# Where the copy of the softmax denominators' row stands in ScalarE's order, inside the block of values and keys

## The chip, the cores and the metric

The kernel runs on one core of a Trainium2 chip. Its engines work side by side, each through its own list of instructions in order: TensorE (PE in the profile, its weight loads PEld) multiplies matrices into PSUM, ScalarE (ACT) applies functions and copies, VectorE (DVE) does elementwise work, GpSimd (POOL) the same[...], and SyncE (SP) issues transfers. They wait for one another by semaphores. The metric is the device time of one execution in microseconds. Before the change it is 2444.21 us, the median of 3 runs (2444.15 to 2444.86).

## The reference

Two layers, each followed by a residual and a layer norm, on x of 16 batches x 1024 nodes x 256 channels. The first layer makes a weighted adjacency from the channel means, its queries from that graph, and runs attention with 4 heads of 64:

```python
c_adj = jnp.mean(fea, axis=1)                       # fea = x transposed
diff = c_adj[:, None, :] - c_adj[:, :, None]
A = jnp.abs(jnp.abs(jax.nn.sigmoid(diff) - 0.5) - 0.5) * 2.0
A_s = (A + jnp.transpose(A, (0, 2, 1))) * 0.5
Wg = adj[None, :, :] * A_s
g = jax.nn.relu(jnp.einsum('bcn,bnm->bcm', fea, Wg) * para.reshape(1, C, N))
q = ...                                             # g, split in heads
kv = (x @ kv_w)...                                  # keys and values, split in heads
attn = jax.nn.softmax(jnp.einsum('bhnd,bhmd->bhnm', q, k) * scale, axis=-1)
out = jnp.einsum('bhnm,bhmd->bhnd', attn, v)
x = _layernorm(x + out)
```

The second layer aggregates x over the normalised adjacency, applies two matmuls with batch norms and a relu, and ends in the same residual and layer norm. The change concerns the first layer alone.

## The kernel before, in words

The first layer is a software pipeline over units of attention. A unit is one batch, one pair of heads, one half of the queries (512) and one chunk of 128 keys: 32 units a batch. `scores` (L1053) multiplies keys by queries into PSUM and ScalarE takes the exponent (L1058); `outputs` (L1074) multiplies values by it, while VectorE adds the exponents up in `acc` (L1082, L1084). Two units form a burst, so a batch b has bursts u = 0 to 15. The loop over bursts writes out by hand the order of the instructions of TensorE, ScalarE, VectorE and SP: nothing is moved by a scheduler afterwards, and an instruction at the head of an engine's list holds all behind it.

Between the bursts the loop places the work that prepares batch b + 1 and finishes batch b - 1. It is kept in lists of steps, and `run(list, k)` emits the next k of them.

- `steps` holds values (L995) and keys (L982) in turn: `values(0), keys(0,0), values(1), keys(0,1), values(2), keys(1,0), values(3), keys(1,1)`. Each fills one PSUM tile of 128 x 512 with four or two matmuls, and is then copied to SBUF: keys by ScalarE (L986), values 1 and 3 by ScalarE and values 0 and 2 by VectorE (L1000).
- `side` holds the graph weights in 8 chunks of 128 x 1024: `weights_abs` (L827, ScalarE, |c_m - c_n|), `weights_tanh` (L832, ScalarE) and `weights_adj` (L836, VectorE, times adj).
- `sums` holds `normalise`: four matmuls with ones (L1122) add the partial exponents over the partitions into a PSUM tile `den`, ScalarE copies it to `drow` (L1128), and SP stores its four rows (L1130) and loads them back as columns (L1135). The column's reciprocal (L1143) later scales the attention output on GpSimd (L1149, L1150).
- `rows_of` holds the four SP loads (L1113) that bring an attention output back in rows.

Values, keys and `den` take their PSUM tiles in turn from one pool of two buffers: the tile after next waits until the copy out of the present one is done. So `den` sits between keys(0,0) and values(1), and keys(0,1) reuses the buffer that `den` has left.

The block of values and keys is burst u = 0 of batches 1 to 14 (in batch 0 the lists are empty, and batch 15 takes another branch). It emits seven of the eight values and keys, with the denominators of the second pair of heads of batch b - 1 after the second:

```python
for i in range(7):
    if b:
        run(steps, 1)
        run(side, (2, 3, 2, 3, 2, 2, 99)[i])
    if i == 1:
        run(sums, 1)
        run(rows_of, 1)
```

When the block starts, seven entries of `side` have been emitted in bursts 9 to 15 of the batch before. The next are tanh 3 and abs 4 (with i = 0), then tanh 4, adj 0 and abs 5 (with i = 1), then tanh 5 and adj 1, and so on.

Of the kernel before, what the change touches and what calls it, by code (L numbers as in the profile page):

```python
# [515 lines left out]
def fast_path(  # L516
# [218 lines left out]
    with (  # L735
# [36 lines left out]
        def load_rest():  # L772
            for n in range(2, NCH, 2):
                nc.sync.dma_start(adj_s[:, n : n + 2, :], adj_src[:, n : n + 2, :])
                if n == 2:
                    load_x(1)
            nc.sync.dma_start(para_s, para.rearrange("o (c p) i j -> p (o c) (i j)", p=P))
# [395 lines left out]
        def run(fs, k):  # L1173
            for f, a in fs[:k]:
                f(*a)
            del fs[:k]
# [135 lines left out]
        with tc.manual_schedule(  # L1312
            engines={
                mybir.EngineType.PE, mybir.EngineType.Activation, mybir.EngineType.DVE,
                mybir.EngineType.SP,
            }
        ):


            first, steps, side = prologue(0)  # L1320
            run(first, 5)
            load_rest()
            next_first, next_steps, next_side = prologue(1)
            for i in range(8):
                run(steps, 1)
                if i > 3:
                    run(side, 2)
                if i == 6:
                    run(next_first, 1)
                    load_squares(1, 0)  # L1330
            run(side, 99)
            for n in range(NCH):
                run(steps, 1)
                if n in (1, 5):
                    run(next_first, 1)
                if n == 1:
                    load_squares(1, 1)
                if n:
                    run(next_side, 3)
            for _ in range(8):  # L1340
                run(next_steps, 1)
                run(next_side, 1)
            full, sums, late = [], [], []
            rows_of = []

            def back(j):

                for i in bursts[j]:
                    outputs(i)
                b, pr, qh, m = units[bursts[j][-1]]  # L1350
                if m == NCH - 1 and qh == 1:
                    sums.append((normalise, (b, pr)))
                    for q in range(2):
                        full.append((residual, (b, pr, q)))
                    if pr == PAIRS - 1:
                        for f in (statistics_x1, finish_x1):
                            for ns in (range(NCH // 2), range(NCH // 2, NCH)):
                                late.append((f, (b, ns)))

            last, before_last = {}, {}  # L1360
            for u, todo in (
                (6, (load_x1l, 0)), (7, (load_weights,)), (9, (degrees,)), (10, (row_of_degrees,)),
                (11, (transpose_weights, 0)), (12, (transpose_weights, 1)),
                (13, (add_identity,)), (14, (scale_adjacency, 0)),
            ):
                last.setdefault(u, []).append((todo[0], todo[1:]))
            for f, places in (
                (transpose_adjacency, (9, 11, 13, 15, 17, 19, 21, 23)),
                (load_adjacency_squares, (6, 9, 9, 11, 13, 15, 17, 19)),
                (adjacency_columns, (11, 13, 14, 16, 18, 20, 22, 24)),  # L1370
            ):
                for m, u in enumerate(places):
                    where = before_last if u < PERB else last
                    where.setdefault(u % PERB, []).append((f, (m,)))
            for u, n in ((9, 6), (10, 7)):
                before_last.setdefault(u, []).append((adjacency_rows, (n,)))
            for i in range(4):
                ns = range(2 * i, 2 * i + 2)
                last.setdefault(8 + i, []).append((statistics_x1, (B - 2, ns)))
            for u, ns in ((13, range(2)), (14, range(2, 5)), (15, range(5, NCH))):  # L1380
                last.setdefault(u, []).append((finish_x1, (B - 2, ns)))
            last[15].append((load_x1l, (1,)))
            for j in range(len(bursts)):
                b, u = j // PERB, j % PERB
                for i in bursts[j]:
                    scores(i)
                if u == 0:
                    steps, side = next_steps, next_side
                    next_first, next_steps, next_side = [], [], []
                if j:  # L1390
                    back(j - 1)
                if u in (5, 9, 13):
                    run(rows_of, 1)
                if u == 5 and b + 2 < B:
                    load_x(b + 2)
                    next_first, next_steps, next_side = prologue(b + 2)
                if b == B - 1:
                    if u == 0:
                        run(sums, 1)
                        run(rows_of, 1)  # L1400
                    elif u in (2, 13):
                        run(full, 2)
                    elif u == 8:
                        run(sums, 1)
                    elif u == 3:
                        late.clear()
                elif u == 0:
                    for i in range(7):
                        if b:
                            run(steps, 1)  # L1410
                            run(side, (2, 3, 2, 3, 2, 2, 99)[i])
                        if i == 1:
                            run(sums, 1)
                            run(rows_of, 1)
                elif u < 4:
                    if u == 1:
                        run(full, 2)
                    else:
                        run(late, 1)
                    run(side, 99)  # L1420
                elif u == 4:
                    p = st[b + 1]["graph"]["p"]
                    keys_last = steps[:1] if b else []
                    del steps[: len(keys_last)]
                    p[1]()
                    run(keys_last, 1)
                    run(late, 2)
                    p[2]()
                    p[3]()
                elif u == 8:  # L1430
                    p = st[b + 1]["graph"]["p"]
                    p[6]()
                    run(next_first, 1)
                    run(sums, 1)
                    if b == B - 2:
                        adjacency_diagonal()
                        for n in range(6):
                            adjacency_rows(n)
                    p[7]()
                    p[5]()  # L1440
                    p[4]()
                elif u < 8:
                    st[b + 1]["graph"]["between"](u)
                else:
                    if u == 9 and b + 2 < B:
                        load_squares(b + 2, 0)
                    if u == 11:
                        run(full, 2)
                    if u == 12:
                        run(next_first, 1)  # L1450
                        if b + 2 < B:
                            load_squares(b + 2, 1)
                    if u == 15:
                        run(next_first, 1)
                    run(next_side, 1)
                if b == B - 2:
                    run(before_last.get(u, []), 9)
                if b == B - 1:
                    run(last.get(u, []), 9)
            j = len(bursts)  # L1460
            back(j - 1)
            for m in range(NCH):
                if m == 0:
                    for k in range(3, NCH):
                        scale_adjacency(k)
                elif m < 4:
                    adjacency_sums(m - 1)
                elif m == 4:
                    adjacency_sums(3)
                aggregate_first(m)  # L1470
                if m == 1:
                    run(sums, 1)
                if m == 4:
                    run(full, 2)
            late.clear()
            x_last = st.pop(B - 1)["x"]
            last_statistics, last_apply = layernorm_steps(x_last, f"l0_{B - 1}")
            last_statistics()
# [583 lines left out]
```

## Time and profile before

| what | value |
|---|---|
| median of 3 runs | 2444.21 us |
| the profiled execution | 2444.04 us |
| its span on the core | 2442.3 us |
| TensorE busy | 2401.4 us, 98% of the span |
| VectorE busy | 1860.5 us, 76% |
| ScalarE busy | 1239.0 us, 51% |
| GpSimd busy | 462.8 us, 19% |
| granted TensorE clock | 0.997 |

The span is what the trace covers; the profiled execution's own time lies 1.7 us above it. Each line of a profile group gives the source line, the engine, the operation, out<-in with shapes and count, then the busy time, the mean of one in ns, and the idle time just before them with what ended it. In the time line the first column is the start in us, the second the stretch that the merged instructions cover. A time line's merged rows of one engine may overlap a little, since a matmul's end is modelled. TensorE's matmuls in 32 bits appear as two records each.

### The profile page before, as it was taken

How to read it: one execution, taken by the hardware profiler on the slowest of the kernel's cores; microseconds unless marked ns; L12 is line 12 of the kernel's file. 1: busy time of each engine (PE TensorE's matmuls, PEld its weight loads, DVE VectorE, ACT ScalarE, POOL GpSimd, SP SyncE). 2: the span in 40 equal slices, each digit the busy share in tenths (PEclk: the TensorE clock that was granted, in tenths of full speed). 3: DMA queues.
4: the chain of work that ended last, by engine and by line, in shares of the span. 5: the costliest groups of instructions: out<-in, count | busy, mean ns of one | idle time of the engine just before them, and what ended most of it. 6: DMA issues, size and time to landing. Idle time of an engine off the chain costs nothing.

```text
span 2442.3 us, 32486 instructions
## 1 busy us (share of the span) xinstructions
PE 2401.4 (98%) x12294; PEld 1015.7 (42%) x12294; DVE 1860.5 (76%) x2561; ACT 1239.0 (51%) x1539; POOL 462.8 (19%) x467
## 2 busy tenths in 40 slices
PE   9999999999999999999999999999999999999996
PEld 5343443443434434434344343344444444444444
DVE  5688878878888788788888888955566556479978
ACT  7376675765765756657657667420110111144568
POOL 0021112111211211112112112422122122010026
PEclk9999999999999999999999999999999999999999
DMA  5124232332242332332322326321221221265558
GB/s 164 40 40 87 56 50 70 69 52 65 41 81 57 49 79 61 53 70 53 66 62 40 87 46 92 90 103 69 86 103 69 88 102 69 86 222 177 180 202 357
DMA packets 437877, 221.96 MB, mean 91 GB/s; under 512 B 361552, under 2 KB 411216, under 8 KB 431568
## 3 DMA queue, kind: packets, MB, share of 16 engines
q1 hardware_dynamic: 418400, 169.20, 28.2%
q0 software_dynamic: 2528, 33.57, 3.3%
q10 hardware_dynamic: 16784, 17.04, 2.1%
q8 instruction: 98, 1.61, 0.3%
q14 instruction: 67, 0.55, 0.1%
HBM read 136.06 MB, written 83.69 MB: 90 GB/s over the span
## 4 chain that ended last, share of the span: by engine, by line
PE 86%; DVE 9%; ACT 2%; DMA 1%; issue 1%; POOL 0%; POOLq 0%; DVEq 0%; ACTq 0%
PE ps L1053 18%; PE po L1074 18%; PE pgb L885 7%; PE b_agg L1558 4%; PE pga L885 4%; PE c_agg L1558 4%; PE pk L982 4%; PE b_o L1766 3%; PE pv L995 3%; PE a_agg L1558 2%; PE b_h L1590 2%; PE pgc L885 2%; PE pgd L885 2%; PE c_o L1766 2%; PE a_o L1766 2%; PE c_h L1590 2%
## 5 line engine op out<-in xcount | busy, mean ns | idle before, releaser
L1058 ACT ACTIVATE p<-ps 128x1024 f32<-128x1024 f32 x512 | 497.2, 1021 | 183.8 <-PE ps L1053 146.0
L1084 DVE TENSOR_TENSOR acc<-acc,p 128x1024 f32<-128x1024 f32 x384 | 499.9, 1302 | 53.4 <-ACT p L1058 28.5
L1053 PE MATMUL ps<-qT,kT 64*64 64x512 f32 x4096 | 488.1, 592 | 0.3 <-ACT p L1058 0.3
L1074 PE MATMUL po<-p,v 64*64 64x512 f32 x4096 | 485.3, 589 | 0.0
L1149 POOL TENSOR_TENSOR o<-o,r_all 128x512 f32<-128x512 f32 x62 | 94.8, 1540 | 1162.3 <-DVE r_all L1143 989.0
L1074 PEld LDWEIGHTS po<-p,v 64*64 64x64 f32 x4096 | 158.2, 133 | 281.2 <-issue 274.3
L1053 PEld LDWEIGHTS ps<-qT,kT 64*64 64x64 f32 x4096 | 151.5, 133 | 286.8 <-issue 249.1
L836 DVE SCALAR_TENSOR_TENSOR wg<-wg,adj_s 128x1024 f32<-128x1024 f32 x128 | 149.6, 1216 | 17.6 <-ACT wg L832 17.6
L827 ACT ACTIVATE wg<-crow,ccol 128x1024 f32<-128x1024 f32 x128 | 146.8, 1147 | 0.0
L832 ACT ACTIVATE wg<-wg 128x1024 f32<-128x1024 f32 x128 | 136.0, 1062 | 0.9
L995 PE MATMUL pv<-kvw_s,xT 128*128 128x256 f32 x512 | 125.1, 387 | 0.0
L982 PE MATMUL pk<-xT,kvw_s 128*128 128x512 f32 x256 | 121.9, 598 | 3.1 <-ACT drow L1128 3.1
L995 PEld LDWEIGHTS pv<-kvw_s,xT 128*128 128x128 f32 x512 | 95.7, 191 | 50.3 <-issue 14.2
L895 ACT ACTIVATE qT<-qT 128x512 f32<-128x512 f32 x60 | 37.4, 630 | 156.1 <-DVE qT L898 145.3
L885 PE MATMUL pgb<-wg,S 128*128 128x512 f32 x240 | 111.0, 605 | 0.0
L885 PE MATMUL pga<-wg,x 128*128 128x512 f32 x240 | 109.6, 599 | 0.7 <-ACT qT L908 0.7
L1558 PE MATMUL a_agg<-ahT,x1l 128*128 128x512 f32 x240 | 108.1, 593 | 0.7 <-ACT agg L1300 0.7
L1150 POOL TENSOR_TENSOR x<-x,o 128x512 f32<-128x512 f32 x62 | 107.8, 1749 | 2.4
L1558 PE MATMUL b_agg<-aT,x1S 128*128 128x512 f32 x240 | 107.9, 592 | 0.0
L656 ACT COPY p_agg<-a_agg 128x512 f32<-128x512 f32 x15 | 8.8, 585 | 183.4 <-PE a_agg L1558 183.4
L692 POOL TENSOR_TENSOR x1S<-x1l 128x512 f32<-128x512 f32 x15 | 19.4, 1297 | 353.6 <-PE c_agg L1558 349.6
L1082 DVE TENSOR_TENSOR acc<-p,p 128x1024 f32<-128x1024 f32 x64 | 77.3, 1208 | 7.5 <-ACT p L1058 7.5
(230 smaller groups left out, 3468.5 us busy)
## 6 DMA issues: line engine op xcount, KB each, us to landing
h<-hw POOLq DMA_DIRECT2D x16, 2048.0 KB, 6.7
hl<-h SPq DMA_DIRECT2D x32, 1024.0 KB
x<-x ACTq DMA_DIRECT2D x16, 1024.0 KB
x1l<-x SPq DMA_DIRECT2D x16, 1024.0 KB
xf<-x SPq DMA_DIRECT2D x16, 1024.0 KB
o<-oS SPq DMA_DIRECT2D x62, 256.0 KB
o<-o SPq DMA_DIRECT2D x248, 64.0 KB
x<-in_x_dram SPq DMA_DIRECT2D x15, 1024.0 KB
```

Source lines behind the costliest of these rows:

```text
L827: nc.scalar.activation(w, s["crow"], AF.Abs, bias=s["ccol"][:, n : n + 1])
L832: nc.scalar.activation(w, w, AF.Tanh, scale=0.5)
L836: nc.vector.scalar_tensor_tensor(w, w, 1.0, adj_s[:, n, :], op0=ALU.subtract, op1=ALU.mult)
L885: nc.tensor.matmul(ps, left, right, start=(start and i == 0), stop=(i == NCH // 2 - 1), skip_group_check=True,)
L982: nc.tensor.matmul(ps, kvw_s[:, c, kc * P : (kc + 1) * P], s["xT"][:, c, hs], start=(c == 0), stop=(c == CC - 1),)
L995: nc.tensor.matmul(pt[:, j * C : (j + 1) * C], s["xT"][:, c, n * P : (n + 1) * P], kvw_s[:, c, C : 2 * C], start=(c == 0), stop=(c == CC - 1),
L1053: nc.tensor.matmul(ps[kh * D : (kh + 1) * D, hd * HALF : (hd + 1) * HALF], kT[r, pr, ks], qT[r, pr, qh * HALF : (qh + 1) * HALF], start=Tr ...
L1058: nc.scalar.activation(p, ps, AF.Exp)
L1074: nc.tensor.matmul(g["po"][kh][hd * D : (hd + 1) * D, :], s["v"][r, m, h * D : (h + 1) * D], p[r, hd * HALF : (hd + 1) * HALF], start=(m = ...
L1084: nc.vector.tensor_add(g["acc"], g["acc"], p)
L1558: nc.tensor.matmul(ps, left, right, start=(start and i == 0), stop=(i == NCH // 2 - 1), skip_group_check=True,)
L1766: nc.tensor.matmul(ps, left, right, start=(start and i == 0), stop=(i == 1), skip_group_check=True,)
```

## The change

The row copy of the block of values and keys, on ScalarE, is emitted after the tanh of chunk 4 and before the abs of chunk 5; until now it came after that abs. The block's second step emits one entry of `side` (tanh 4) in place of three, then come the denominators and the loads of rows, and then the two entries held back (adj 0, abs 5).

```diff
                     for i in range(7):
                         if b:
                             run(steps, 1)
-                            run(side, (2, 3, 2, 3, 2, 2, 99)[i])
+                            run(side, (2, 1, 2, 3, 2, 2, 99)[i])
                         if i == 1:
                             run(sums, 1)
                             run(rows_of, 1)
+                            run(side, 2 if b else 0)
```

Engine by engine, the built programs differ in ScalarE's order alone, in 14 places, one for each of the batches 1 to 14: `tanh 4, abs 5, drow, v` becomes `tanh 4, drow, abs 5, v`. No instruction is added or taken away.

## The prediction

> **What bounds the kernel now.** I read the page first: busy shares, the chain that ended last, then the group of the matmuls beside the edit.
>
> ```profile
> PE 2401.4 (98%) x12294; PEld 1015.7 (42%) x12294; DVE 1860.5 (76%) x2561; ACT 1239.0 (51%) x1539; POOL 462.8 (19%) x467
> PE 86%; DVE 9%; ACT 2%; DMA 1%; issue 1%; POOL 0%; POOLq 0%; DVEq 0%; ACTq 0%
> L982 PE MATMUL pk<-xT,kvw_s 128*128 128x512 f32 x256 | 121.9, 598 | 3.1 <-ACT drow L1128 3.1
> ```
>
> TensorE is busy for 98% of the span and is 86% of the last chain, so a microsecond that TensorE stands still is, very nearly, a microsecond of the kernel. ScalarE has time to spare; it matters only where TensorE waits for it. The third line is such a place: the key matmuls wait for the copy that the change moves. Asked for that copy alone, the trace says who waited for it (us, times):
>
> ```profile
>   PEld pk L982: 8.8, 14
>   PE pk L982: 3.1, 14
> ```
>
> Fourteen waits: one in the block of values and keys of each of the batches 1 to 14. 8.8/14 = 0.63 us is the idle time of the weight load, 3.1/14 = 0.22 us that of the multiplier. Neither is yet the true loss, because matmul ends are modelled and loads overlap. For that I read the time line of one such block (batch 7), first up to the wait:
>
> ```profile
> 730.28 1.99 PE L995 MATMUL pv<-kvw_s,xT 128*128 128x256 f32 x8
> 732.12 1.88 PE L982 MATMUL pk<-xT,kvw_s 128*128 128x512 f32 x4
> 733.93 1.06 PE L1122 MATMUL den<-acc,ones 128*32 128x512 f32 x8
> 734.03 0.59 ACT L986 COPY kT<-pk 128x512 f32<-128x512 f32 x1 [1.05 <-PE pk L982]
> 734.52 1.06 ACT L832 ACTIVATE wg<-wg 128x1024 f32<-128x1024 f32 x1
> 734.92 1.99 PE L995 MATMUL pv<-kvw_s,xT 128*128 128x256 f32 x8
> 735.47 1.14 ACT L827 ACTIVATE wg<-crow,ccol 128x1024 f32<-128x1024 f32 x1
> 736.51 0.57 ACT L1128 COPY drow<-den 128x512 f32<-128x512 f32 x1
> 736.98 0.60 ACT L1000 COPY v<-pv 128x512 f32<-128x512 f32 x1
> ```
>
> and then after it:
>
> ```profile
> 737.14 0.30 PEld L982 LDWEIGHTS pk<-xT,kvw_s 128*128 128x128 f32 x2 [0.62 <-ACT drow L1128]
> 737.14 1.98 PE L982 MATMUL pk<-xT,kvw_s 128*128 128x512 f32 x4 [0.22 <-ACT drow L1128]
> 737.46 1.07 ACT L832 ACTIVATE wg<-wg 128x1024 f32<-128x1024 f32 x1
> 738.96 1.89 PE L995 MATMUL pv<-kvw_s,xT 128*128 128x256 f32 x8
> 739.16 0.58 ACT L986 COPY kT<-pk 128x512 f32<-128x512 f32 x1 [0.63 <-PE pk L982]
> 740.47 0.41 PEld L982 LDWEIGHTS pk<-xT,kvw_s 128*128 128x128 f32 x2
> 740.69 1.88 PE L982 MATMUL pk<-xT,kvw_s 128*128 128x512 f32 x4
> 742.40 1.89 PE L995 MATMUL pv<-kvw_s,xT 128*128 128x256 f32 x8
> ```
>
> The denominators' matmuls (den) end at 734.99. ScalarE is then inside a tanh until 735.58, goes on to an abs, and copies the row only at 736.51 to 737.08. The next key matmuls reuse den's PSUM buffer, and start at 737.14, 0.06 us after that copy. All that time the row stood ready.
>
> **What the Trainium skill says.** "TensorE: Matmul & The Clock Gate", Step-by-step: matmuls stay in program order, and the next weight load is pulled ahead of the matmul in flight. The trace agrees: the undisturbed pair loads at 740.47, 0.22 us before its matmul at 740.69; the held pair loads and starts together at 737.14, so its load is bare. "ScalarE: Activation LUTs", Table sets: cheap functions are in every set, and tanh is with exp. So copy, tanh and abs in another order should want no table load; the trace has such sequences back to back without a gap (kT copy 734.03, tanh 734.52, abs 735.47). The same page, What ACT_TABLE_LOAD costs, has back-to-back activations overlap by about 93 ns: here the tanh ends at 735.58 and the abs starts at 735.47, 0.11 us.
>
> **The change part by part.**
> Removed and added: no instruction; counts and tiles stay. On ScalarE, one order changes 14 times: tanh of chunk 4, abs of chunk 5, row copy becomes tanh of chunk 4, row copy, abs of chunk 5. The multiplication by adj that the code moves with the abs is VectorE's, and has no other VectorE instruction to change places with; VectorE, TensorE and the DMA queues keep their orders. Batch 0 has no such block, batch 15 takes another branch: both cost nothing.
>
> The copy: it takes the abs's place at 735.47 and ends near 736.05, 1.04 us sooner. It needs den, done at 734.99, so it does not wait (0.48 us spare). Its release reaches TensorE at about 736.11. Without a wait, the key matmuls would follow their values as the first pair of the block does: 730.28 to 732.12, 1.84 us. So they start at 734.92 + 1.84 = 736.76, with a load 0.22 us ahead at 736.54, still 0.43 us after the release. The wait is gone.
>
> What that is worth: the held step took 737.14 - 734.92 = 2.22 us, the free one 1.84: 0.38 us. The held key matmuls then take 738.96 - 737.14 = 1.82 us to the next values, the free ones 742.40 - 740.69 = 1.71: 0.11 us for the bare load. Together 0.49 us. The blocks of batch 1 (154.77, 156.98, 158.81) and batch 14 (1411.78, 1413.99, 1415.81) give 2.21 and 1.83 or 1.82 in the same places, so 0.48 to 0.50. I take 0.49: 14 x 0.49 = 6.9 us. The bounds are the profile's two rows, 3.1 us (multiplier's idle time) and 8.8 us (load's); the lower leaves out the bare load and the modelled end, the upper counts 0.2 us in which the load would have rested anyway.
>
> The abs of chunk 5: it starts about 0.47 us later (735.94). Queued behind it are the copy of values (v), the tanh of chunk 5, the next kT copy. But abs plus row copy is the same sum either way, so v still starts near 736.98, where its own matmuls have just ended (734.92 + 1.99 = 736.91), and the tanh at 737.46. So VectorE gets chunk 5 no later. Hidden: nothing to pay.
>
> Next possible waits, with TensorE 0.49 us ahead: the third values' load moves from 738.53 to 738.04, and needs v, done at 737.58: 0.40 us spare after 0.06 of signal. The kT copy follows its matmuls (ScalarE idles 0.63 us for them); its tanh ends at 738.53, the keys then at about 738.6: 0.1 us spare. Third keys, load at 739.98, need that kT copy, done near 739.25. From there every ScalarE and VectorE step waits for TensorE, and moves with it.
>
> DMAs: the copy's four stores, four column loads and the four loads of rows queued behind them on SP start up to 1.04 us sooner (stores from 737.11 to about 736.07). SP has nothing else waiting there; the reciprocal at 748.18 that uses them is held by VectorE's own order. Worth nothing here.
>
> The batches are in lockstep, 96.70 us apart, so what a block gains is not given back by a fixed clock; no TensorE wait for a DMA is listed after the start.
>
> Sum: the profiled execution took 2444.04 us (span 2442.3 and 1.7 around it); minus 6.9 is 2437.1. The median of the runs is 0.17 above it: 2444.21 - 6.9 = 2437.3.
>
> **The rivals.**
> Only the multiplier's named idle time comes back: 14 x 0.22 = 3.1 us, 2441.1. For it: that is how the profile prices the wait. Against: the starts of the matmuls, which are not modelled, show 0.49.
>
> The wait moves on: the next values wait for v, or the keys for kT, by what was gained: 2444.2. For it: the smallest of these margins is 0.1 us. Against: that smallest one delays ScalarE alone; TensorE's own margins are 0.4 us or more.
>
> Slower: the row copy, now ahead of the abs, finds den unfinished and stops ScalarE's queue, as in the middle of each batch, where the copy waited up to 4.1 us. Place: row copy at 735.47. v comes 1.51 us after it, lasts 0.60, signals in 0.06, and is needed at 738.04, so it hurts from a den later than 735.87, eats the gain by 736.36, and costs 0.2% (0.35 us in each block) from 736.7. At 737.0: 14 x (1.13 - 0.49) = 9 us, 2453. Against: den ends at 734.99, 0.9 us before the first of these points, and its place on TensorE is unchanged.
>
> That the order doesn't change can be left out: it is ScalarE's own program order.
>
> **How the numbers follow.** About 0.2%, 4.9 us, is what a measurement of this kernel can tell from no change. The forecast (0.43 to 0.62 us a block) has 0.84; its own range is 2435.5 to 2438.2. Multiplier's share only 0.07, wait moved on 0.06, slower 0.03. Faster by over 0.2%: 0.84 and a little of the partial cases, 0.86; within: 0.11; slower: 0.03. The range runs from the whole load wait, 2444.2 - 8.8 = 2435.4, to the multiplier's share alone, 2441.1.
>
> **What would show it.** In the profile after, no key matmul waits for drow; values to keys takes about 1.84 us, keys to the next values 1.71; the batch period falls from 96.70 to 96.2; ScalarE's row copy starts right after the tanh with no wait for den. Wrong: a wait of values for v or of drow for den in these blocks, or a period that shrinks by 0.2.

## The result, and the profile after

The changed kernel takes 2437.33 us, the median of 9 runs (2436.02 to 2437.80), against 2444.15 us, the median of 9 runs of the kernel before (2442.96 to 2444.86). The ratio is 0.9971 with a 95% interval of 0.9961 to 0.9982, so 6.8 us less, and clear of no change. The forecast was 2437.3 us. The profiled execution took 2437.42 us, its span 2435.6 us, 6.7 us less than the span before.

The page after: the engines' busy time, the chain that ended last, and the group of the key matmuls.

```profile
PE 2397.9 (98%) x12294; PEld 1016.6 (42%) x12294; DVE 1860.0 (76%) x2561; ACT 1239.0 (51%) x1539; POOL 462.9 (19%) x467
PE 89%; DVE 9%; DMA 1%; issue 1%; ACT 0%; SPq 0%; POOL 0%; DVEq 0%; POOLq 0%; ACTq 0%
L982 PE MATMUL pk<-xT,kvw_s 128*128 128x512 f32 x256 | 120.4, 592 | 0.0
```

The same work is done: counts are equal, and the busy time of ScalarE is the same to 0.1 us. What went is the idle time ahead of the keys, 3.1 us before and 0.0 now, and with it ScalarE's 2% of the last chain. That share is not the gain. In every block before, the chain ran through tanh, abs and row copy, 1.06 + 1.03 + 0.48 = 2.57 us in batch 7, or 36 us in 14 blocks, and the span lost 6.7: TensorE was at work beside them for most of that time. In the trace after, nobody waits for the row copy.

The time line of the block of batch 7, from den on (columns as before: start, stretch, engine, line, operation, and in brackets the idle time before it):

```profile
730.18 1.06 PE L1122 MATMUL den<-acc,ones 128*32 128x512 f32 x8
730.77 1.06 ACT L832 ACTIVATE wg<-wg 128x1024 f32<-128x1024 f32 x1
731.17 1.99 PE L995 MATMUL pv<-kvw_s,xT 128*128 128x256 f32 x8
731.73 0.58 ACT L1128 COPY drow<-den 128x512 f32<-128x512 f32 x1
732.19 1.16 ACT L827 ACTIVATE wg<-crow,ccol 128x1024 f32<-128x1024 f32 x1
732.79 0.41 PEld L982 LDWEIGHTS pk<-xT,kvw_s 128*128 128x128 f32 x2
733.01 1.88 PE L982 MATMUL pk<-xT,kvw_s 128*128 128x512 f32 x4
733.24 0.58 ACT L1000 COPY v<-pv 128x512 f32<-128x512 f32 x1
733.71 1.08 ACT L832 ACTIVATE wg<-wg 128x1024 f32<-128x1024 f32 x1
734.72 1.89 PE L995 MATMUL pv<-kvw_s,xT 128*128 128x256 f32 x8
734.92 0.58 ACT L986 COPY kT<-pk 128x512 f32<-128x512 f32 x1
```

From values 1 to the keys it is now 733.01 - 731.17 = 1.84 us, where it was 2.22; from the keys to values 2 it is 734.72 - 733.01 = 1.71 us, where it was 1.82. The weight load of the keys stands 0.22 us ahead of its matmul again (732.79), hidden behind the values. That is 0.49 us in this block.

It recurs in all of them. The chain that ended last shows the first graph product of each batch; these are those of batches 2, 3 and 4, in the kernel before and then in the changed one:

```profile
178.03 3.63 PE pga L885 x8
274.73 3.63 PE pga L885 x8
371.42 3.63 PE pga L885 x8
```

```profile
176.74 3.63 PE pga L885 x8
272.94 3.63 PE pga L885 x8
369.14 3.63 PE pga L885 x8
```

96.70 us a batch have become 96.20. Fourteen times 0.49 us is 6.9 us, and so it is over all the blocks together: from the first graph product of batch 1 to that of batch 15 the chain takes 1435.04 - 82.11 = 1352.93 us before and 1427.36 - 81.31 = 1346.05 after. The spans differ by 6.7 us. The rest is not the change's: in this pair of executions the graph product of batch 1, ahead of all the blocks, already starts 0.8 us sooner (81.31 for 82.11), and what follows the blocks takes about a microsecond more.

### The profile page after: what moved, and what is told of

Read it like the earlier page. It is cut to its first block, busy times and chain, and to the rows that moved or that the text cites. A ratio compares the mean times of both kernels' runs of the same rounds, so it can differ in the third digit from the quotient of the medians.

```text
span 2435.6 us, 32486 instructions
## 1 busy us (share of the span) xinstructions
PE 2397.9 (98%) x12294; PEld 1016.6 (42%) x12294; DVE 1860.0 (76%) x2561; ACT 1239.0 (51%) x1539; POOL 462.9 (19%) x467
## 4 chain that ended last, share of the span: by engine, by line
PE 89%; DVE 9%; DMA 1%; issue 1%; ACT 0%; SPq 0%; POOL 0%; DVEq 0%; POOLq 0%; ACTq 0%
PE ps L1053 18%; PE po L1074 18%; PE pgb L885 7%; PE b_agg L1559 5%; PE pv L995 4%; PE pga L885 4%; PE c_agg L1559 4%; PE pk L982 4%; PE b_o L1767 3%; PE a_agg L1559 2%; PE b_h L1591 2%; PE pgc L885 2%; PE pgd L885 2%; PE c_o L1767 2%; PE a_o L1767 2%; PE c_h L1591 2%
```

## The experiments

All times are medians; each ratio is against runs of the kernel before on the same chip.

| kernel | what differs from before | us (runs) | before, us | ratio, 95% interval |
|---|---|---|---|---|
| changed | row copy ahead of abs 5 | 2437.33 (9) | 2444.15 | 0.9971 [0.9961, 0.9982] |
| e1_odd | the same in 7 of the 14 blocks | 2440.72 (21) | 2444.14 | 0.9986 [0.9979, 0.9992] |
| e2_later | row copy behind tanh 5 | 2458.94 (5) | 2444.14 | 1.0061 [1.0047, 1.0075] |
| e3_earlier | row copy ahead of tanh 4 | 2437.35 (8) | 2444.14 | 0.9972 [0.9962, 0.9983] |
| e4_own_buffer | order of before, den in another PSUM pool | 2437.23 (9) | 2444.14 | 0.9973 [0.9963, 0.9983] |
| e5_both | changed order and e4's pool | 2437.21 (8) | 2443.97 | 0.9972 [0.9962, 0.9983] |

**Half of the blocks.** The changed order in the odd batches alone:

```diff
-                            run(side, (2, 3, 2, 3, 2, 2, 99)[i])
+                            run(side, (2, 1 if b % 2 else 3, 2, 3, 2, 2, 99)[i])
                         if i == 1:
                             run(sums, 1)
                             run(rows_of, 1)
+                            run(side, 2 if b % 2 else 0)
```

> The new order in the odd batches alone, 7 blocks of 14. Theory (each block's key matmuls wait for the row copy, 0.49 us a block, and nothing else changes): 7 x 0.49 = 3.4 us below before, about 2440.7; the listed wait of keys for drow is left 7 times, and the distance from block to block alternates between 96.2 and 96.7. Rival (a shift of the whole schedule, won or lost once): 2437.3 or 2444.2.

Measured: 3.4 us less than before. Who waited for the row copy, and the starts of the graph products of batches 2 to 5 in the chain that ended last:

```profile
  PEld pk L982: 4.4, 7
  PE pk L982: 1.6, 7
```

```profile
176.71 3.63 PE pga L885 x8
273.40 3.63 PE pga L885 x8
369.60 3.63 PE pga L885 x8
466.30 3.63 PE pga L885 x8
```

The distances are 96.69, 96.20, 96.70: long where the order is the old one, short where it is new. The gain is made block by block, about half a microsecond in each, and is kept. The rival, a shift won once, falls.

**One place later.** The row copy behind the tanh of chunk 5:

```diff
-                            run(side, (2, 3, 2, 3, 2, 2, 99)[i])
+                            run(side, (2, 4, 1, 3, 2, 2, 99)[i])
```

> The row copy one place later than before, after the tanh of chunk 5 (the copy of values 1 stays right behind it). Theory (TensorE pays one for one for every us that the row copy is late): tanh before it starts at abs + 1.04, the copy 0.97 us later than before, so keys 0.97 us later in each block: 14 x 0.97 = 13.6 us above before, about 2457.8. Rival (the chunk of weights that comes earlier for VectorE counts too): less than 10 us above.

Measured: 14.8 us more than before, 1.2 us beyond the theory's figure. Batch 7 in the time line:

```profile
740.93 1.99 PE L995 MATMUL pv<-kvw_s,xT 128*128 128x256 f32 x8
741.48 1.14 ACT L827 ACTIVATE wg<-crow,ccol 128x1024 f32<-128x1024 f32 x1
742.65 1.06 ACT L832 ACTIVATE wg<-wg 128x1024 f32<-128x1024 f32 x1
743.62 0.57 ACT L1128 COPY drow<-den 128x512 f32<-128x512 f32 x1
744.24 1.99 PE L982 MATMUL pk<-xT,kvw_s 128*128 128x512 f32 x4 [1.31 <-ACT drow L1128]
```

The tanh starts 1.17 us after the abs, not 1.04. It reads what the abs writes, and 742.65 is after the abs ends at 742.62, where instructions that don't depend on each other overlapped by 0.1. The block of batch 7 in the kernel before, further on, already had such a pair, 1.18 us apart:

```profile
739.64 1.15 ACT L827 ACTIVATE wg<-crow,ccol 128x1024 f32<-128x1024 f32 x1
740.82 1.06 ACT L832 ACTIVATE wg<-wg 128x1024 f32<-128x1024 f32 x1
```

An exponent that doesn't read the abs ahead of it starts 1.04 us after it there (706.56 to 707.60), so it is not the abs, nor a change of function alone, that takes the overlap away. So the row copy comes 743.62 - 741.48 = 2.14 us after the start of the abs, where it was 1.04 (735.47 to 736.51): 1.10 us later. The keys start 744.24 - 740.93 = 3.31 us after the values, where it was 2.22: 1.09 us later. Fourteen times 1.09 is 15.3 us, and from the first graph product of batch 1 to that of batch 15 the chain is 15.2 us longer than before (81.60 to 1449.74); the medians differ by 14.8. TensorE pays one for one once it is held. The theory's 0.97 was off by the overlap that a dependent pair doesn't have. The rival, that VectorE's earlier chunk pays some of it back, isn't seen.

**One place earlier.** The row copy ahead of the tanh of chunk 4:

```diff
-                            run(side, (2, 3, 2, 3, 2, 2, 99)[i])
+                            run(side, (2, 0, 2, 3, 2, 2, 99)[i])
                         if i == 1:
                             run(sums, 1)
                             run(rows_of, 1)
+                            run(side, 3 if b else 0)
```

> The row copy one place earlier than in the changed kernel, ahead of the tanh of chunk 4. Theory: ScalarE is free for it at 734.5 and must wait for den until 735.0, so 0.4 to 0.5 us of ScalarE's queue is lost; tanh, abs and the copy of values 1 come 0.5 us later than in the changed kernel, that copy ends near 738.1 where its buffer's next weight load is wanted at 738.04: a hold of 0.1 us and a bare load of 0.1, so 0.1 to 0.25 us a block are given back: 2438.7 to 2440.8, and the page lists a wait of values for v. Rival (earlier is never worse, TensorE has slack there): 2437.3, no such wait.

Measured: 2437.35 us, the same as the changed kernel. The theory missed. Batch 7:

```profile
731.16 0.59 ACT L1128 COPY drow<-den 128x512 f32<-128x512 f32 x1 [0.43 <-PE den L1122]
731.64 1.06 ACT L832 ACTIVATE wg<-wg 128x1024 f32<-128x1024 f32 x1
732.60 1.14 ACT L827 ACTIVATE wg<-crow,ccol 128x1024 f32<-128x1024 f32 x1
732.85 1.88 PE L982 MATMUL pk<-xT,kvw_s 128*128 128x512 f32 x4
733.64 0.57 ACT L1000 COPY v<-pv 128x512 f32<-128x512 f32 x1
734.26 1.79 PEld L995 LDWEIGHTS pv<-kvw_s,xT 128*128 128x128 f32 x8 [0.36 <-ACT v L1000]
734.57 1.89 PE L995 MATMUL pv<-kvw_s,xT 128*128 128x256 f32 x8
```

Everything on ScalarE came as foretold: it waits 0.43 us for den, v ends at 734.21, and the load of values 2 starts at 734.26, held for 0.36 us where the free one rests for 0.24. So it is late by 0.12 us, and yet the matmuls of values 2 start 734.57 - 732.85 = 1.72 us after the keys, as in the changed kernel. The free load starts 0.43 us ahead of its matmul here (738.53 against 738.96 in the kernel before) and lasts 0.19; the late one starts 0.31 us ahead, still in the shadow of the keys. The profile lists this wait in all 14 blocks, 5.1 us in total, and none of it shows in the time. The theory had taken the start of the undisturbed load for the latest that costs nothing.

**Another buffer, the old order.** In the blocks of batches 1 to 14, the tile of den comes from the pool of the attention outputs:

```diff
-            den = tile_s("den_last")[:, H0] if last else tile_t(f"den_{k}")
+            tile = tile_o if pr == 1 and b < B - 2 else tile_t
+            den = tile_s("den_last")[:, H0] if last else tile(f"den_{k}")
```

> ScalarE's order as before; the denominators' PSUM tile of these blocks alone is taken from the pool of the attention outputs, which rests there, so no key matmul needs the buffer that the row copy frees. Theory (the loss is the buffer's reuse alone): the whole gain comes back, 14 x 0.49 = 6.9 us, and up to 0.1 us a block more, since values 1 no longer reuse the keys' buffer and their load need not be bare: 2435.9 to 2437.3. Rival (the gain comes from the row's transfers that start sooner, or from the later abs): none of these moves here, 2444.2.

Measured: 6.9 us less than before. Batch 7 (the row copy is line 1129 here):

```profile
730.81 1.06 PE L1123 MATMUL den<-acc,ones 128*32 128x512 f32 x8
731.81 1.59 PEld L995 LDWEIGHTS pv<-kvw_s,xT 128*128 128x128 f32 x8 [0.84 <-issue]
731.81 1.99 PE L995 MATMUL pv<-kvw_s,xT 128*128 128x256 f32 x8
732.36 1.14 ACT L827 ACTIVATE wg<-crow,ccol 128x1024 f32<-128x1024 f32 x1
733.40 0.57 ACT L1129 COPY drow<-den 128x512 f32<-128x512 f32 x1
733.64 1.88 PE L982 MATMUL pk<-xT,kvw_s 128*128 128x512 f32 x4
735.36 1.89 PE L995 MATMUL pv<-kvw_s,xT 128*128 128x256 f32 x8
```

The abs is ahead of the row copy as in the kernel before, and the copy still runs when the keys start: 1.83 us after the values, 1.72 to the next. ScalarE's order, the abs's place and the time at which the row is stored are those of before, and the gain is all there. So the changed order gains nothing by moving those, and the reuse of den's buffer is the whole loss. The extra 0.1 us for values 1 didn't come: without any wait for a ScalarE copy their load still starts with the matmul, 1.00 us after den (before, 734.92 - 733.93 = 0.99). The 0.84 us that the profile before lists there as a wait of this load for the kT copy cost nothing. Why the load isn't pulled ahead of den's matmuls, these runs don't show.

**Both together.** The changed order with this pool.

> The changed order and the denominators' own buffer together. Theory (both take away the same wait, and the run with the own buffer left the load of values 1 after den as it was): nothing more than either alone, 2437.3 within a microsecond, block to block 96.20 us, no wait for drow listed. Rival (two different losses, each worth 6.9): 2430.4.

Measured: 2437.21 us, no more than either alone. Its block distance is 96.20 us, and no wait for the row copy is listed. The two edits take away the same 0.49 us, and none of the five kernels beats the changed one by more than its own runs scatter.

## Why the prediction was right

The forecast case came in, and its steps can be read one by one in the profile after. That the median, 2437.33, lies within 0.1 us of the forecast 2437.3 is luck, since the runs scatter from 2436.02 to 2437.80; that the 14 blocks together gave 6.9 us is not.

- *The row copy takes the abs's place and doesn't wait for den.* It starts 0.56 us after values 1 (731.73 - 731.17), where the abs had started 0.55 us after them, with no idle time listed.
- *The keys start 1.84 us after the values, with a hidden load; 0.38 and 0.11 us come back.* 1.84 and 1.71 as forecast. Both terms were needed: the multiplier's idle time that the profile lists, 0.22 us a block, would have given 3.1 us. Half of the blocks (3.4 us for 7) and the whole (6.8 us for 14) both give 0.49 us each. The rival of the named idle time falls.
- *The abs's later start is hidden.* v starts 2.07 us after its values began (733.24 - 731.17); before it was 2.06 (736.98 - 734.92). The own buffer, which left the abs where it was, came to the same time.
- *The wait doesn't move on.* The kT copy had 0.1 us to spare by forecast; the tanh before it ends at 734.79, the copy starts at 734.92. No wait of values for v is listed.
- *Transfers that start sooner are worth nothing.* The row's stores are issued 1.16 us after values 1 began (732.33), where it was 2.19 (737.11); with its own buffer they stay late (2.19, 734.00), and the kernel is as fast.
- *The slower rival.* Its mechanism, the row copy stopping ScalarE at an unfinished den, was brought about one place earlier: ScalarE stood 0.43 us and TensorE lost nothing. So the point from which it hurts was put too early: the prediction took it that the load of values 2 must start by 738.04, and it can come at least 0.12 us later for nothing. The rival would have needed a den still later than stated; how much later wasn't tried.

The range was as wide as the profile's two rows of idle time, 3.1 and 8.8 us. The starts of the matmuls in three blocks, 0.48 to 0.50 us each, would have given 6.7 to 7.0 us, narrower than the scatter of the runs.

## What to carry to other kernels

Where a small PSUM pool turns over, look at which copy frees the buffer that the bottleneck wants next, and put that copy ahead of work on its engine whose result isn't wanted yet; a tile from a pool that is at rest did the same here. Price such a wait from the starts of the held matmuls against an undisturbed pair in the same block, not from the idle time that the profile lists: that was 0.22 us a block for a loss of 0.49, and 0.36 us a block for none with the row copy one place earlier. Once the buffer came in time, coming earlier was worth nothing.

## What the runs showed of the hardware that was not expected

A weight load that was held for a short time cost nothing: 0.12 us late (0.31 us ahead of its matmul in place of 0.43), it left the matmul where it was. Fully bare, starting with its matmul, it cost 0.11 us. The values show nearly the same: with their bare load in the run where den has its own buffer they take 733.64 - 731.81 = 1.83 us to the keys, and the third values of the kernel before, whose load comes early, 740.69 - 738.96 = 1.73. And on ScalarE the overlap of back-to-back instructions, 0.1 us here, was missing where the second read what the first wrote: the tanh started 1.17 us after the abs of its own chunk, the row copy 1.04 us after an abs that it doesn't read.
